# Masking x1 instead of the adjacency in a two-layer graph kernel, with other buffers and new orders

## Chip, core and metric

The kernel runs on one core of one Trainium2 chip. Its time is the device time of a run in microseconds (us); a version is described by the median of several runs. In the profile PE is TensorE (matmuls), PEld its weight load, DVE is VectorE, ACT is ScalarE, POOL is GpSimd and SP the engine that issues transfers. The operands of the products are 32-bit floats.

## What is computed

There are 64 graphs of 256 nodes with 512 features. Layer 0 averages the neighbours, multiplies by a weight and normalises; layer 1 scores each node by a product of queries and aggregated keys, takes a softmax of the scores over the nodes, adds the values so weighted, and normalises again.

```python
def layer0(x, adj, W):
    deg = jnp.sum(adj, axis=-1, keepdims=True)
    agg = jnp.einsum('bij,bjf->bif', adj, x) / jnp.maximum(deg, EPS)
    cat = jnp.concatenate([x, agg], axis=2)
    return jax.nn.relu(jnp.einsum('bnf,of->bno', cat, W))

def layer1(X, adj, mask, Wqk, Wv):
    q, k = jnp.split(X @ Wqk, 2, axis=-1)
    v = X @ Wv
    k_m = k * mask[:, :, None]
    agg = jnp.einsum('bij,bjd->bid', adj, k_m)
    w = inv_scale * mask * jnp.einsum('bid,bid->bi', q, agg)
    return jax.nn.softmax(w, axis=1)[:, :, None] * v

x = layernorm(x + layer0(x, adj, W))
x = layernorm(x + layer1(x, adj, nodemask, Wqk, Wv))
```

The mask stands on the node that is summed over: masking row j of the keys is the same as masking column j of the adjacency, or row j of x1, the input of layer 1, since the key weights can be multiplied in after the aggregation.

## The kernel before

Graphs go in pairs, 32 of them, and a loop over pairs j computes layer 0 of pair j together with layer 1 of pair j-1. Each product of 256x512 by 512x512, and each aggregation of 256x256 by 256x512, is done by Winograd's form of Strassen's method: seven products of half size and some sums of blocks on either side. Six of the seven weight products are split once more in the same way (seven matmuls of 256 columns), one is not (four matmuls of 512 columns, two for each graph).

Layer 0 consists of the products named i, k, m, p, q, r, s (`layer0`) and the gather a to g: the aggregation, applied to y, which is x times the second half of the weight. Layer 1 consists of J, K, H, Q, N, P, L (`layer1`), and the gather A to G, the aggregation of x1. The key weights were multiplied into the query weights at the start, so the scores are the dot product of q with the aggregate, and no product with keys remains. A gather needs the sums S1 to S4 of the adjacency (`adj_sums`, on GpSimd) and T1 to T4 of the other operand (`sums_T`, on VectorE). For layer 0, T1 of y comes out of the copy from PSUM (`split`), and T2 to T4 go to a buffer of their own, `tv`. For layer 1 the four T sums are made from x1 (`owns[j]`) and written to the first half of the buffer `shared` (`agg_of`). The aggregate takes the place of the T sums there, block by block, as the gather's matmuls have read them.

The mask is applied to the adjacency (`mask_adj`, four ScalarE instructions on 256 columns) once layer 0 has used it, and `adj_sums` is made a second time, from the masked adjacency, into the second of two buffers `sa`.

The buffer `turn` (`turned_rows`) has three uses in turn: rows of the adjacency, of which `degrees` takes the row sums on ScalarE (in place, two graphs by two halves); the transposed x1, which 16 transfers on SP's queue place in x1T (`norm0`, `place`); and the scores of all nodes on each partition, for the softmax.

The order of the work is made in two steps. `ORDER0` (first pair), `ORDER1` (second), `ORDER` (all others) and `ORDER9` (layer 1 of the last pair) name the TensorE units in the order in which they are recorded; `take` goes through them, and each `when` adds the work on other engines once the units that it names have been taken. An inner product has seven units, the whole one four, a gather unit has two matmuls, one for each graph. Then `Plan` arranges all recorded instructions anew: it has a cost for each, gives each a due time (TensorE's own position in the recorded order, and for the other engines what is needed for that), and lists, engine by engine, the ready instruction with the earliest due time. The program is issued in that order, and every engine then works through its list in order. `HOME` and `HOME9` name the PSUM bank in which a product or a gather unit works; the whole products use no such bank. `FULL_FIRST` and the like name products that are done whole at the start and the end. L is the last product of layer 1; `ahead` carries units of it from one pair to the next, if the order leaves some: with the strings of before it leaves none. `softmax` and the sums of layer 1 start when L is done (`start_layer1`).

All engine instructions have the line of one helper, 285 in the profile; matmuls have 370, transposes 376, transfers 386. Groups are told apart by the names of their tiles.

Of the kernel before, what the change touches and what calls it, by code (L numbers as in the profile page):

```python
# [13 lines left out]
OP = mybir.AluOpType  # L14
# [15 lines left out]
HOME = "i6 k7 m7 p2 q6 r7 s6 a7 b2 c3 J3 K2 H1 Q5 N7 L7 P7 A6 B4 C5"  # L30
HOME9 = "J1 K7 H3 Q7 N6 L1 P1 A2 B3 C1"
# [4 lines left out]
ORDER0 = ("k i k i k i i k i k i i k p k p m m m m q q s m m p p r r m r q r r r s r q a b s s d e c f g")  # L36
ORDER1 = ("i k i i k i i i i k k k p m m k k m m p m p q m m r p r r q r q q q q r q s r s s r s s a J J J "
          "J J s b s d e c J J f H K K H Q H K H K K K Q Q g N N K A N D P Q C E G N N N N P P L L L B L P "
          "L F L L")
ORDER = ("i k i i i k k i k i k i k m k p p p m m q m m r p r r m m r r r q q r q q q J q s J J s s s J J "  # L40
         "s a b d s s J e c J H f K K H K H g K K H K K Q Q A N Q N Q Q D N N C Q Q N P N E P N P P G P P "
         "P L F L B L L L L L")
ORDER9 = ("J J J J A J J C J D K B K K H K E H F G N H N H K Q Q K N P N N Q N Q N P K P P L S L Z L L")
# [277 lines left out]
def resnorm_kernel(  # L321
# [58 lines left out]
    def send(out, in_, due=None, late=0.0):  # L380
# [8 lines left out]
    (adjs, rows, xs, Xs, rdegs, sumsA, sumsM, owns, ys, aggs, vs, x1Ts, scores, columns, rows_w,  # L389
     probs) = ({} for _ in range(16))  # L390

    shared = mem.tile([P, 4 * N_SIDE], F32, name="shared")
# [4 lines left out]
    turned_rows = mem.tile([P, 2 * NT * F], F32, name="turn")  # L397
# [12 lines left out]
    def load_rows(j):  # L410
        rows[j] = turned_rows[:, :2 * NT * N].rearrange("p (k t n) -> p k t n", k=2, t=NT)
        for k in range(2):
            send(rows[j][:, k], adj[2 * j + k].rearrange("(t p) j -> p t j", p=P), late=LATE if j else 0.0)
# [113 lines left out]
    def adj_sums(j, n):  # L527
        a, s = adjs[j], sa[n]
# [6 lines left out]

    def mask_adj(j):
        for k in range(2):
            for t in range(NT):
                act.activation(adjs[j][:, k, t], adjs[j][:, k, t], AF.Copy,
                               scale=mask_sb[:, 2 * j + k, t:t + 1])  # L540
# [88 lines left out]
    def sums_T(val, to=None):  # L629
        b11, b12, b21, b22 = (val[:, :, t, h * HF:(h + 1) * HF] for t in range(NT) for h in range(2))  # L630
        if to is None:
            tv = ring("tv", [P, 3, 2, HF])
            t2, t3, t4 = (tv[:, r] for r in range(3))
            t1 = b12
        else:
# [512 lines left out]
```

## Time and profile before

| what | value |
|---|---|
| three runs | 1818.59, 1818.78, 1822.25 us; median 1818.78 |
| the profiled execution's own time | 1818.37 us |
| its span, first to last instruction | 1816.6 us |
| granted TensorE clock | 0.999 |
| HBM | 82 GB/s over the span |

The span is what the profile covers; the execution's own time is 1.8 us longer. Shares of busy time are means over the whole span: the first 110 us, in which weights are multiplied and summed and the pipeline fills, and the last 20 us, in which only one pair's layer 1 is left, look different from the loop between them. In a row of instruction groups the columns are line, engine, operation, output and inputs by name, shapes and count, then busy time in us and the mean of one in ns, then the idle time before them and what ended it. In an order of time the first two columns are the start and the duration in us; "x2" stands for two records, and a matmul on 32-bit floats has two.

The transfers of one pair in the loop, in order of time (start, duration over all that were merged, and how many):

```profile
499.55 11.26 SPq L386 DMA_DIRECT2D x1T<-turn  x16
510.91 0.56 SPq L386 DMA_DIRECT2D dram<-turned  x1
511.57 0.90 SPq L386 DMA_DIRECT2D turn<-adj  x2
513.25 0.37 SPq L386 DMA_DIRECT2D turn<-dram  x1
526.54 6.36 SPq L386 DMA_DIRECT2D xT<-x_t  x2
```

First the 16 that place x1T, then the scores' way through DRAM and the adjacency rows for the degrees of the next pair.

### The profile page before, as it was taken

What the parts mean: (1) busy time and instruction counts of PE and PEld (TensorE: products, weight loads), DVE (VectorE), ACT (ScalarE), POOL (GpSimd) and SP (SyncE); (2) the same over time, 40 slices, a digit from 0 to 9 for tenths busy, and PEclk for the clock granted to TensorE, in tenths of its full rate; (3) what the DMA queues carried; (4) which work ended last, traced back from release to release, by engine and by line L of the source; (5) the groups of instructions that cost most, each with busy time, mean ns of one, the idle gap of its engine ahead of it and who ended that gap; (6) DMA issues with size and microseconds to landing.
All of it is one profiled execution on the core that took longest, in us unless ns stands there. A gap on an engine that the chain in (4) does not pass through costs nothing.

```text
span 1816.6 us, 27899 instructions
## 1 busy us (share of the span) xinstructions
PE 1801.9 (99%) x7724; PEld 1439.9 (79%) x7724; DVE 1562.1 (86%) x3511; ACT 1299.2 (72%) x3475; POOL 1196.6 (66%) x1729
## 2 busy tenths in 40 slices
PE   9999999999999999999999999999999999999998
PEld 5777878878888888878788788888788887788875
DVE  7888888889888889898888898898888888988886
ACT  3657876678766778766787767787667777667866
POOL 5866676766766866766767667667667666676652
PEclk9999999999999999999999999999999999999999
DMA  7134334343243443343433433433434333334312
GB/s 239 52 77 116 94 94 100 99 111 101 86 117 87 101 118 95 91 112 88 111 104 97 104 88 100 122 94 88 119 81 111 106 104 95 97 92 120 94 20 77
DMA packets 380730, 181.72 MB, mean 100 GB/s; under 512 B 263712, under 2 KB 345248, under 8 KB 380576
## 3 DMA queue, kind: packets, MB, share of 16 engines
q1 hardware_dynamic: 380576, 179.94, 36.7%
q8 instruction: 63, 1.03, 0.3%
q14 instruction: 91, 0.75, 0.1%
HBM read 114.35 MB, written 34.08 MB: 82 GB/s over the span
## 4 chain that ended last, share of the span: by engine, by line
PE 98%; DVE 1%; DMA 1%; ACT 0%; SPq 0%; issue 0%; ACTq 0%; DVEq 0%
PE bank L370 98%; DMA shared<-wqk_t 1%; DVE bank L285 0%; PE bank L376 0%; DVE own L285 0%; SPq L386 0%; ACT own L285 0%; DVE t_i L285 0%; DVE st L285 0%; DVE w L285 0%; DVE x L285 0%; DVE y L285 0%; ACT y L285 0%; ACT shared L285 0%; DVE top L285 0%
## 5 line engine op out<-in xcount | busy, mean ns | idle before, releaser
L285 DVE TENSOR_TENSOR bank<-bank,fifth 128x256 f32<-128x256 f32 x866 | 377.9, 465 | 119.0 <-ACT fifth L285 83.1
L285 ACT COPY fifth<-bank 128x256 f32<-128x256 f32 x616 | 220.0, 373 | 234.1 <-PE bank L370 232.8
L285 ACT COPY y<-bank 128x512 f32<-128x512 f32 (+1 forms) x256 | 135.5, 532 | 130.8 <-PE bank L370 112.3
L370 PE MATMUL bank<-t_i,x1T_i 128*128 128x256 f32 x748 | 207.5, 379 | 1.1 <-ACT bank L285 1.1
L285 ACT COPY shared<-bank 128x512 f32<-128x512 f32 x314 | 179.8, 594 | 36.9 <-PE bank L370 34.8
L285 ACT ACTIVATE own<-own,shift,rstd 128x512 f32<-128x512 f32 x254 | 201.0, 828 | 0.2 <-DVE shift L285 0.2
L370 PE MATMUL bank<-t_i,xT_i 128*128 128x256 f32 x760 | 195.9, 379 | 0.0
L285 DVE SCALAR_TENSOR_TENSOR own<-bank,rdeg,own 128x256 f32<-128x256 f32 x384 | 172.2, 477 | 19.3 <-PE bank L370 17.0
L285 ACT ACTIVATE junk<-own,less 128x512 bf16<-128x512 f32 x254 | 184.0, 724 | 3.1
L285 ACT COPY bank<-bank 128x256 f32<-128x256 f32 (+1 forms) x352 | 145.9, 421 | 54.9 <-PE bank L370 35.8
L370 PEld LDWEIGHTS bank<-t_i,x1T_i 128*128 128x128 f32 x748 | 140.8, 190 | 35.6 <-issue 9.0
L285 DVE TENSOR_TENSOR y<-bank,y 128x512 f32<-128x512 f32 (+1 forms) x256 | 150.6, 618 | 20.2 <-PE bank L370 17.6
L370 PE MATMUL bank<-t,x1T_s 128*128 128x512 f32 (+1 forms) x384 | 163.5, 521 | 0.6 <-DVE own L285 0.6
L285 POOL TENSOR_TENSOR shift<-less,rstd 128x2 f32<-128x2 f32 x126 | 23.1, 203 | 212.9 <-ACT rstd L285 212.6
L370 PEld LDWEIGHTS bank<-t_i,xT_i 128*128 128x128 f32 x760 | 140.4, 189 | 27.4 <-issue 1.9
L370 PE MATMUL bank<-t,xT_s 128*128 128x512 f32 (+1 forms) x384 | 159.7, 521 | 0.0
L285 DVE TENSOR_TENSOR shared<-bank,shared 128x512 f32<-128x512 f32 (+1 forms) x157 | 138.4, 883 | 9.5 <-ACT shared L285 6.8
L285 POOL TENSOR_TENSOR x1T_i<-x1T 128x256 f32<-128x256 f32 x124 | 97.2, 793 | 74.8 <-PE bank L370 71.8
L370 PE MATMUL bank<-w,x1T_i 128*128 128x256 f32 x500 | 144.5, 380 | 0.5 <-DVE bank L285 0.5
L370 PE MATMUL bank<-w,xT_i 128*128 128x256 f32 x508 | 141.2, 380 | 0.6 <-DVE bank L285 0.5
L285 POOL TENSOR_TENSOR xT_s<-xT,xT_s 128x256 f32<-128x256 f32 x62 | 65.3, 1070 | 112.2 <-PE bank L370 110.8
L285 POOL TENSOR_TENSOR sa<-adj 128x256 f32<-128x256 f32 x128 | 92.1, 729 | 59.2 <-ACT adj L285 55.0
(174 smaller groups left out, 4788.5 us busy)
## 6 DMA issues: line engine op xcount, KB each, us to landing
x<-x SPq DMA_DIRECT2D x64, 512.0 KB, 3.4
xT<-x_t SPq DMA_DIRECT2D x62, 512.0 KB, 3.3
out<-own SPq DMA_DIRECT2D x62, 512.0 KB, 3.4
x1T<-turn SPq DMA_DIRECT2D x480, 64.0 KB, 2.1
turn<-adj SPq DMA_DIRECT2D x64, 256.0 KB, 3.3
adj<-adj_t SPq DMA_DIRECT2D x64, 256.0 KB, 3.5
turn<-dram SPq DMA_DIRECT2D x31, 264.0 KB, 5.1
shared<-wqk_t SPq DMA_DIRECT2D x4, 512.0 KB, 8.4
```

The source lines that it names most:

```text
L285: self.plan.record(self.name, lambda: call(out, *args, **kwargs), outs, ins, busy, done, port)
L370: plan.record("PE", lambda: nc.tensor.matmul(ps, a, b, start=start, stop=True, skip_group_check=True), [ps], [a, b], busy, busy + 0.165, w ...
```

## The change

- `mask_adj` and the second `adj_sums` are gone. `adj_sums` is made once for a pair, into one of the two buffers `sa` in turn, and used by both gathers.
- In their place `masked_T` masks x1: two ScalarE copies a graph write the masked blocks B11 (256 columns), and B21 with B22 (512 columns), to a new buffer `masked`. T1 is one VectorE instruction a graph (mask times block, less B11); T2, T3 and T4 are three GpSimd subtractions over both graphs. T still goes to the first half of `shared`. B12 isn't copied: T1 reads it from x1 itself and masks it on the way.
- `sums_T` now serves y alone, and its T2 to T4 go to the front of `turn` instead of `tv`, which is dropped. `turn` grows from 2048 to 2064 columns and the scores' row moves behind the T sums.
- The adjacency rows for the degrees go to `shared` (the first 1024 columns, the aggregate of one graph) from pair 3 on; those of pairs 0 to 2 stay in `turn`.
- `HOME` differs for p and H, which use no such bank. In `HOME9` J's bank changes from 1 to 7; H, Q, L and their like are whole there.
- New strings for all four orders. In `ORDER` the seven units of L are split: one is carried into the next pair, as its ninth unit. The first pairs' and the last one's orders differ in many places.

```diff
@@ -27,20 +27,20 @@
 W1_BY_GP = ("P5", "P3", "P4")
-HOME = "i6 k7 m7 p2 q6 r7 s6 a7 b2 c3 J3 K2 H1 Q5 N7 L7 P7 A6 B4 C5"
-HOME9 = "J1 K7 H3 Q7 N6 L1 P1 A2 B3 C1"
+HOME = "i6 k7 m7 p5 q6 r7 s6 a7 b2 c3 J3 K2 H4 Q5 N7 L7 P7 A6 B4 C5"
+HOME9 = "J7 K7 H2 Q5 N6 L7 P1 A2 B3 C1"
 LATE = 4.0
...
 FULL_FIRST = ("P7", "P4")
-ORDER0 = ("k i k i k i i k i k i i k p k p m m m m q q s m m p p r r m r q r r r s r q a b s s d e c f g")
-ORDER1 = ("i k i i k i i i i k k k p m m k k m m p m p q m m r p r r q r q q q q r q s r s s r s s a J J J "
-          "J J s b s d e c J J f H K K H Q H K H K K K Q Q g N N K A N D P Q C E G N N N N P P L L L B L P "
-          "L F L L")
-ORDER = ("i k i i i k k i k i k i k m k p p p m m q m m r p r r m m r r r q q r q q q J q s J J s s s J J "
-         "s a b d s s J e c J H f K K H K H g K K H K K Q Q A N Q N Q Q D N N C Q Q N P N E P N P P G P P "
-         "P L F L B L L L L L")
-ORDER9 = ("J J J J A J J C J D K B K K H K E H F G N H N H K Q Q K N P N N Q N Q N P K P P L S L Z L L")
+ORDER0 = ("i k i k k i i k k i i i p k k m m m p q m p p m r r q s r r q m r r r q s a s s m b d e c g f")
+ORDER1 = ("k k i k i i i i i k k k i m m m p k m p p m q p m m q r r r q r r r r q q q q s J a J s J s b J "
+          "J s s s s d J e c f J H H Q H K K K K Q H K g N N K Q Q P K N A D C E G B N N N N L P L L P L L "
+          "P F L")
+ORDER = ("i i i k k k k i L i k i k i m k p m m m p m q p p r r r r r m r m r q q q q q J q J s a J J s s "
+         "J s s s s J b d e c J f H K K K H H g K H K K K A Q N Q N Q N Q Q N Q C Q N P P P D E N F N P P "
+         "P G L P B L L L L L")
+ORDER9 = ("J J J C A J J D E B G N J N N J F H K H K N H Q Q K H K P Q N P K Q N K K P N P S L L Z L L")
@@ -386,15 +386,17 @@
-    (adjs, rows, xs, Xs, rdegs, sumsA, sumsM, owns, ys, aggs, vs, x1Ts, scores, columns, rows_w,
-     probs) = ({} for _ in range(16))
-
+    (adjs, rows, xs, Xs, rdegs, sumsA, owns, ys, aggs, vs, x1Ts, scores, columns, rows_w,
+     probs) = ({} for _ in range(15))
+
+    masked = mem.tile([P, 2, 3, HF], F32, name="masked")
     shared = mem.tile([P, 4 * N_SIDE], F32, name="shared")
...
                        for n in ("xT", "x1T"))
-    turned_rows = mem.tile([P, 2 * NT * F], F32, name="turn")
+    N_T, N_ROW = 3 * 2 * HF, P // Q * 2 * NT * (Q + 1)
+    turned_rows = mem.tile([P, N_T + N_ROW], F32, name="turn")
@@ -408,7 +410,7 @@
     def load_rows(j):
-        rows[j] = turned_rows[:, :2 * NT * N].rearrange("p (k t n) -> p k t n", k=2, t=NT)
+        rows[j] = (shared if j > 2 else turned_rows)[:, :2 * NT * N].rearrange("p (k t n) -> p k t n", k=2, t=NT)
         for k in range(2):
@@ -524,20 +526,14 @@
-    def adj_sums(j, n):
-        a, s = adjs[j], sa[n]
+    def adj_sums(j):
+        a, s = adjs[j], sa[j % 2]
         a11, a21, a12, a22 = (a[:, :, t, h * P:(h + 1) * P] for t in range(2) for h in range(2))
...
         return {"A11": a11, "A12": a12, "A22": a22, "S1": s[:, 0], "S2": s[:, 1], "S3": s[:, 2], "S4": s[:, 3]}
-
-    def mask_adj(j):
-        for k in range(2):
-            for t in range(NT):
-                act.activation(adjs[j][:, k, t], adjs[j][:, k, t], AF.Copy,
-                               scale=mask_sb[:, 2 * j + k, t:t + 1])
@@ -626,23 +622,30 @@
-    def sums_T(val, to=None):
+    def masked_T(j):
+
+        t1, t2, t4, t3 = (aggs[j][:, :, t, h * HF:(h + 1) * HF] for t in range(NT) for h in range(2))
+        b11, b21, b22 = (masked[:, :, r] for r in range(3))
+        x1 = owns[j]
+        for k in range(2):
+            m = mask_sb[:, 2 * j + k]
+            act.activation(b11[:, k], x1[:, k, 0, :HF], AF.Copy, scale=m[:, 0:1])
+            act.activation(masked[:, k, 1:].rearrange("p r f -> p (r f)"), x1[:, k, 1], AF.Copy, scale=m[:, 1:2])
+            vec.scalar_tensor_tensor(t1[:, k], x1[:, k, 0, HF:], m[:, 0:1], b11[:, k],
+                                     op0=OP.mult, op1=OP.subtract)
+        gp.tensor_sub(t2, b22, t1)
+        gp.tensor_sub(t3, t2, b11)
+        gp.tensor_sub(t4, b21, t2)
+        return {"B11": b11, "B21": b21, "B22": b22, "T1": t1, "T2": t2, "T3": t3, "T4": t4}
+
+    def sums_T(val):
         b11, b12, b21, b22 = (val[:, :, t, h * HF:(h + 1) * HF] for t in range(NT) for h in range(2))
-        if to is None:
-            tv = ring("tv", [P, 3, 2, HF])
-            t2, t3, t4 = (tv[:, r] for r in range(3))
-            t1 = b12
-        else:
-            t1, t2, t4, t3 = (to[:, :, t, h * HF:(h + 1) * HF] for t in range(NT) for h in range(2))
-        if to is not None:
-            vec.tensor_sub(t1, b12, b11)
-        vec.tensor_sub(t2, b22, t1)
-        if to is None:
-            vec.tensor_sub(t3, t2, b11)
-        else:
-            vec.tensor_sub(t3, b22, b12)
+        tv = turned_rows[:, :3 * 2 * HF].rearrange("p (r k f) -> p r k f", r=3, k=2)
+        t2, t3, t4 = (tv[:, r] for r in range(3))
+        vec.tensor_sub(t2, b22, b12)
+        vec.tensor_sub(t3, t2, b11)
         vec.tensor_sub(t4, b21, t2)
-        return {"B11": b11, "B21": b21, "B22": b22, "T1": t1, "T2": t2, "T3": t3, "T4": t4}
+        return {"B11": b11, "B21": b21, "B22": b22, "T1": b12, "T2": t2, "T3": t3, "T4": t4}
@@ -757,7 +760,7 @@
         x1Ts[j] = Side(home_x1, *sums_x1, 1, SLOTS_X1)
-        sq = turned_rows.rearrange("p (b k c t q) -> p b k c t q", b=P // Q, k=2, c=NF, t=NT)
+        sq = turned_rows[:, :2 * NT * F].rearrange("p (b k c t q) -> p b k c t q", b=P // Q, k=2, c=NF, t=NT)
@@ -793,7 +796,7 @@
         send(d, turned)
-        row = turned_rows[:, NT * F:NT * F + P // Q * 2 * NT * (Q + 1)].rearrange("p (a c) -> p a c", a=P // Q)
+        row = turned_rows[:, N_T:].rearrange("p (a c) -> p a c", a=P // Q)
         send(row, d.rearrange("(a c) q -> a c q", c=Q)[:, :2 * NT, :].rearrange("a c q -> a (c q)")
@@ -925,7 +928,7 @@
     inner_sums(Xs[0], "P2")
-    sumsA[0] = adj_sums(0, 0)
+    sumsA[0] = adj_sums(0)
     degrees(0)
@@ -947,12 +950,11 @@
         def start_gather0():
-            units.update(gather("abcdefg", sumsA.pop(j), sums_T(ys[j]), at["a"], at["c"], at["b"],
+            units.update(gather("abcdefg", sumsA[j], sums_T(ys[j]), at["a"], at["c"], at["b"],
                                 own=own, rdeg=rdegs.pop(j)))
...
             place = norm0(j)
-            mask_adj(j)
             if place:
@@ -974,7 +976,7 @@
                 load_adj(j + 1)
-                sumsA[j + 1] = adj_sums(j + 1, 0)
+                sumsA[j + 1] = adj_sums(j + 1)
         if j > 0:
@@ -1011,16 +1013,14 @@
                         turn_here(Y, owns[0], k, o)
-                    mask_adj(0)
                 else:
                     softmax(j - 2)
-                sumsM[j - 1] = adj_sums(j - 1, 1)
                 inner_sums(Y, None)
...
             def start_gather1():
-                units.update(gather("ABCDEFG", sumsM.pop(j - 1), T[0], at["A"], at["C"], at["B"],
+                units.update(gather("ABCDEFG", sumsA.pop(j - 1), T[0], at["A"], at["C"], at["B"],
                                     aggs[j - 1]))
@@ -1029,7 +1029,7 @@
             T = []
-            when("ikmpqrs" if j == 1 else "", lambda: T.append(sums_T(owns[j - 1], aggs[j - 1])))
+            when("ikmpqrs" if j == 1 else "", lambda: T.append(masked_T(j - 1)))
             when("gK", start_gather1)
@@ -1048,8 +1048,7 @@
     aggs[j] = agg_of(j)
-    T = sums_T(x1, aggs[j])
-    sumsM[j] = adj_sums(j, 1)
+    T = masked_T(j)
     turn_here(X, x1, 1, pw)
@@ -1057,7 +1056,7 @@
     units, dots = layer1(j, X, q_at, o, u, y, at)
-    units.update(gather("ABCDEFG", sumsM.pop(j), T, at["A"], at["C"], at["B"], aggs[j]))
+    units.update(gather("ABCDEFG", sumsA.pop(j), T, at["A"], at["C"], at["B"], aggs[j]))
     v = vs[j]
```

## The prediction

> **What bounds the kernel now.** I read the totals of the page first, then the chain of waits, then the busy time of each engine by stretches, and last the order of time around the places where TensorE stood still.
>
> ```profile
> span 1816.6 us, 27899 instructions
> ...
> PE 1801.9 (99%) x7724; PEld 1439.9 (79%) x7724; DVE 1562.1 (86%) x3511; ACT 1299.2 (72%) x3475; POOL 1196.6 (66%) x1729
> ...
> PE 98%; DVE 1%; DMA 1%; ACT 0%; SPq 0%; issue 0%; ACTq 0%; DVEq 0%
> ```
>
> TensorE is busy for 1801.9 of 1816.6 us and holds 98% of the chain that ended last. So 14.7 us is all that work off TensorE can give back, unless matmuls go; the change has the same matmuls (seven gather units of two matmuls before and after). The stretches say where the 14.7 us lie:
>
> ```profile
> core 0: us, PE busy (x) PEld busy (x) DVE busy (x) ACT busy (x) POOL busy (x), PEclk, DMA share, GB/s
> 0.00:55.00 55.00, 52.79 (x172) 31.73 (x173) 41.11 (x74) 22.04 (x62) 35.00 (x50) 1.00 0.66 221
> 55.00:110.00 55.00, 51.56 (x209) 36.80 (x209) 46.59 (x92) 34.29 (x81) 37.83 (x52) 1.00 0.12 39
> ...
> 495.00:550.00 55.00, 55.00 (x240) 44.69 (x239) 47.98 (x109) 40.20 (x110) 37.06 (x54) 1.00 0.39 102
> 525.00:535.00 10.00, 10.00 (x44) 8.03 (x43) 9.91 (x26) 8.64 (x27) 0.87 (x3) 1.00 0.28 96
> ...
> 1760.00:1816.60 56.60, 47.68 (x200) 34.52 (x198) 39.13 (x92) 42.15 (x109) 14.70 (x26) 0.96 0.19 61
> ```
>
> Idle TensorE: 2.2 us in the first stretch, 3.4 in the second, 8.9 in the last, 0 in a stretch of the steady loop. A busy TensorE isn't TensorE at its peak, so its pace counts too. The same matmul of two successive pairs starts at
>
> ```profile
> 500.32 0.59 PE L370 MATMUL bank<-own,sa 128*128 128x256 f32 x2
> ...
> 555.64 0.59 PE L370 MATMUL bank<-own,sa 128*128 128x256 f32 x2
> ```
>
> a period of 55.32 us. In the order of time, starts of 256-column matmuls run from 537.51 to 544.85 in 17 steps, 0.432 us each; two 512-column ones stand between 44.74 and 46.46, 0.86 each. A pair needs, for each of two layers, six products of 7 small matmuls, one of 4 large, and 14 small for the gather: 2 x (56 x 0.432 + 4 x 0.86) = 55.26. So 0.1 us a pair is lost: 29 like pairs, at most 3 us. The 3.4 us of the second stretch are four waits, while the pipeline fills:
>
> ```profile
> 89.65 0.70 PE L370 MATMUL bank<-tv,adj 128*128 128x256 f32 x2 [1.25 <-DVE own L285]
> 90.93 0.70 PE L370 MATMUL bank<-t,x1T_s 128*128 128x256 f32 x2 [0.58 <-DVE own L285]
> ...
> 93.01 1.13 PE L370 MATMUL bank<-w,x1T_i 128*128 128x256 f32 x4 [0.53 <-DVE bank L285]
> 95.23 0.67 PE L370 MATMUL bank<-t_i,x1T_i 128*128 128x256 f32 x2 [1.09 <-ACT bank L285]
> ```
>
> **The change, by pair of graphs.** Durations are these groups':
>
> ```profile
> L285 DVE SCALAR_TENSOR_TENSOR own<-bank,rdeg,own 128x256 f32<-128x256 f32 x384 | 172.2, 477 | 19.3 <-PE bank L370 17.0 <-ACT own L285 0.9
> ...
> L285 POOL TENSOR_TENSOR sa<-adj 128x256 f32<-128x256 f32 x128 | 92.1, 729 | 59.2 <-ACT adj L285 55.0 <-PE bank L370 4.2
> ...
> L285 ACT ACTIVATE adj<-adj,mask_sb 128x256 f32<-128x256 f32 x132 | 67.5, 517 | 3.6 <-PE bank L370 3.2
> ...
> L285 DVE TENSOR_TENSOR shared<-own 128x512 f32<-128x512 f32 x64 | 44.9, 701 | 1.8
> ...
> L285 POOL TENSOR_TENSOR x1T_s<-x1T 128x512 f32<-128x512 f32 x31 | 39.6, 1278 | 0.3 <-ACT x1T L285 0.3
> ```
>
> Removed: on ScalarE four maskings, 4 x 0.517 = 2.07 us; on GpSimd the second set of four adjacency sums, 0.729 x 2 + 0.737 + 0.781 = 2.98; on VectorE four T sums, 2 x 0.701 + 2 x 0.736 = 2.87.
>
> Added: on ScalarE four masked copies, two of 256 columns at 0.517 and two of 512. For the latter the rows give 0.594 (a plain copy of 512 from PSUM) to 0.828 (the scaling of own, two column operands); a copy grows by 0.22 from 256 to 512, so 0.517 + 0.22 = 0.74. Sum 2.51, **+0.44 a pair**. On VectorE two scalar_tensor_tensor of 256 columns, nearest row 0.477: 0.95, **-1.92**; if each is doubled by a wait, as "tv<-y" shows (minimum 0.681, median 1.372), still -1.0. On GpSimd three subtractions of 512 columns: 1.278 each where undisturbed, 1.653 in the row "x1T_s<-x1T_s,x1T": 3.83 to 4.96; I take the first, since two subtractions of that length stand undisturbed in each pair: **+0.85**.
>
> None of the three engines sets the end of a steady pair (48.0, 40.2 and 37.1 of 55), so I cost these at nothing; what hides them is TensorE's 55. GpSimd has the room in one piece: 0.87 busy in 525 to 535.
>
> One rule speaks against the move. The Trainium skill, "Perfetto Trace Analysis", section "Optimizing Scalar/DVE Operations", says that moving work between VectorE and GpSimd might not help, as they share a read port. The trace shows the price: 1.278 on GpSimd against 0.701, and "tv<-y" at twice its minimum. By the rule VectorE's -1.92 would come to nothing; by the rows about -1.9 stays; either way the end isn't touched.
>
> **Moved buffers.** From the fourth pair on, the adjacency rows for the degrees land in the first half of the aggregate, where T is built. So for one of the two graphs T1 waits for the degrees of the next pair, behind which the chain is: dots that read the aggregate end at 505.4; the two row transfers issue at 511.57, behind the 16 that place x1T (from 499.55, 11.26 us); they land about 3.3 us later; ScalarE's degrees ended at 525.95. Then T1 (0.95) and three subtractions (3.83): 530.8. GpSimd's own next work, "shift", starts at 533.40; the first matmul that reads a T sum is "shared,sa" at 543.98. That leaves 13 us; with 1.653 for each subtraction, 12. Cost nothing; if the rows were 14 us late, each further one would cost 29.
>
> T sums of y now wait for the "turn" buffer. In the loop it is free at about 513 (placing ended at 510.8, and about 2 us to land), they start at 521.1: 8 us of cover. In the first pair they started at 41.23, while the degrees of the second pair, in the same buffer, ran from 42.12 to 43.8. Those rows were issued at 23.09, and ScalarE is busy 22 of the first 55 us, so the degrees can go earlier: 0, at most 2.6 us. The reload for the third pair then waits until TensorE has read the sums (49.7 instead of 43.8); its degrees are used an iteration later.
>
> **Orders.** The four strings are priorities: instructions are listed by what is ready, so matmuls next to each other in a string needn't wait for each other. In the new loop one unit of product L is carried into the next pair, and layer 1's start waits for it: it ends after nine units, 9 x 0.43 = 3.9 us. The sums that follow also need the 16 transfers that place x1T, which take 11.26 us to issue; so nothing. Fill: from -3.4 (all four waits gone) to +3.4 (doubled), its own row being all I have. The weight load before the wait at 95.23 is put down to GpSimd's "t_i"; GpSimd loses four sums in this stage and gets its T work later (the T sums stood at 100.0 to 107.3). I credit that wait alone: -1.1. Loop: from -2.9 (nothing lost) to what rival two costs; VectorE is nearly full where hand-offs are closest and loses 1.92, so a third: -1.0. Tail (the one wait there was 0.9): -0.9 to +0.9, taken as 0.
>
> Sum on the profiled execution's own time: 1818.37 (its span of 1816.6 and 1.8 around it) - 1.1 - 1.0 = 1816.3; the median of the runs is 0.4 above that execution: **1816.7**.
>
> **Rivals.** One, *hand-offs cleared*: fill, loop and tail waits all go: -3.4 - 2.9 - 0.9 = -7.2, 1811.6. For it: everything lost is hand-offs, and VectorE, which releases most of them, gets lighter. Against: they are latencies from one engine to the next, not queues.
>
> Two, *VectorE's full stretch*: T1 must follow the degrees, which ended at 525.95, and VectorE is busy 9.91 us of the 10 from 525 on. Of 0.95 us, 0.09 fits; up to 0.86 pushes evictions that TensorE waits for. Above 0.13 us a pair (29 pairs, 3.6 us) it decides; at half of 0.86, 29 x 0.43 = +12.5: 1831. Against: the 2.87 us taken out stood at 501.9 to 508.2, and T1 can be ordered after 535 with 8 us to spare.
>
> Three, *a longer fill*: the first pair's wait of 2.6 and twice the 3.4: +6.0, 1824.8.
>
> **How the numbers follow.** What a measurement of this kernel can tell from no change is 0.2%, 3.6 us. Forecast 0.50, 1813 to 1821, of it 0.17 below 1815.1 and 0.33 within. Rival one 0.17. Rival two 0.25, three 0.08. So faster 0.34, same 0.33, slower 0.33. Low end 1810, below rival one's value, leaving 0.05 out; the top must take in rival three and the part of rival two up to 0.3 us a pair (8.7): 1826, leaving about 0.13 out.
>
> **What would show it.** Right: period 55.2 to 55.35 us, TensorE 55 of 55 in the loop, ScalarE up 0.4, VectorE down 1.9, GpSimd up 0.9 a pair; the wait near 95 us gone. Rival two: a TensorE wait "<-DVE" once a pair, just after the degrees. Wrong altogether: a matmul reading the new T sums and waiting for GpSimd, or transfers of x1T landing later.

## The result and the profile after

The changed kernel takes 1822.49 us (median of 20 runs, 1821.95 to 1823.18); the kernel before, beside it, 1818.72 (20 runs). The ratio is 1.0018, interval 1.0012 to 1.0023: 3.8 us slower, about the 0.2% that a measurement can tell, where 2 us faster was forecast. The profiled execution took 1822.13 us, its span is 1820.4; that of before was 1816.6. The page of the changed kernel, engines' totals and the chain of waits:

```profile
span 1820.4 us, 27722 instructions
...
PE 1806.7 (99%) x7724; PEld 1441.5 (79%) x7724; DVE 1499.8 (82%) x3447; ACT 1322.4 (73%) x3471; POOL 1197.5 (66%) x1697
...
PE 97%; DVE 1%; ACT 1%; DMA 1%; issue 0%; SPq 0%; POOL 0%; ACTq 0%; DVEq 0%
```

TensorE has the same 7724 matmuls and is still 97% of the chain. VectorE has 62 us less to do, and yet TensorE's busy time grew by 4.8 us: matmuls that wait a little are counted as longer ones. Busy time by stretches, the changed kernel (columns as shown before):

```profile
55.00:110.00 55.00, 54.52 (x224) 39.57 (x224) 48.63 (x100) 37.34 (x95) 38.94 (x50) 1.00 0.14 45
110.00:165.00 55.00, 54.04 (x231) 42.53 (x230) 44.96 (x101) 37.49 (x103) 36.91 (x53) 1.00 0.29 75
...
330.00:1595.00 1265.00, 1264.88 (x5469) 1024.58 (x5468) 1051.78 (x2442) 941.65 (x2481) 849.33 (x1205) 1.00 0.38 101
```

and the loop of the kernel before:

```profile
330.00:1595.00 1265.00, 1265.00 (x5487) 1027.20 (x5486) 1104.62 (x2497) 924.58 (x2489) 852.39 (x1230) 1.00 0.38 102
```

From 55 to 110 us TensorE gained 3 us of busy time (51.56 before). From 110 to 165 it lost 1 (55.00 before). The loop, 330 to 1595, looks full, as before, but holds 5469 matmuls in place of 5487. At 0.216 us for one record of 256 columns, 18 of them are 3.9 us. So the loss is in the loop, where busy time can't show it. The same matmul of two successive pairs, in the changed kernel's order of time:

```profile
512.75 0.66 PE L370 MATMUL bank<-w,xT_s 128*128 128x256 f32 x2
...
568.25 0.66 PE L370 MATMUL bank<-w,xT_s 128*128 128x256 f32 x2
```

The period is 55.50 us, against 55.32 before; over the 21 periods between 346 and 1512 us its mean is 55.50, and single ones are 55.46 to 55.51 with two exceptions (55.74, 55.62).

To see where it goes, I took the starts of TensorE's records and summed what each interval has above its usual pace (0.216 us after a record of 256 columns, 0.429 after one of 512, 0.109 after one of 128). These "lost" microseconds by region (us of the span), for the kernels before and changed and for the experiments below whose loops stay near theirs:

| kernel | 0-60 | 60-110 | 110-165 | 165-330 | 330-1600 | 1600-1772 | after | median of runs |
|---|---|---|---|---|---|---|---|---|
| before | 2.8 | 5.15 | 0.6 | 1.0 | 2.6 | 1.2 | 1.8 | 1818.7 |
| changed | 3.2 | 1.9 | 2.2 | 1.0 | 6.8 | 0.85 | 2.2 | 1822.5 |
| e1 new code, old strings | 3.3 | 1.3 | 2.2 | 0.95 | 6.7 | 6.0 | 4.1 | 1830.5 |
| e2 old code, new strings | 3.4 | 4.25 | 0.6 | 1.4 | 3.4 | 7.75 | 2.5 | 1829.3 |
| e3 old code, new fill | 3.7 | 4.2 | 0.6 | 1.9 | 2.6 | 1.2 | 1.8 | 1818.7 |
| e6 T on GpSimd, order kept | 2.8 | 5.1 | 0.9 | 1.7 | 2.5 | 6.6 | 1.9 | 1827.2 |
| e7 changed, order kept, less work | 3.7 | 1.2 | 2.2 | 1.0 | 7.0 | 0.8 | 2.2 | 1821.9 |
| e8 changed, first block ahead | 3.4 | 4.2 | 1.7 | 3.7 | 18.2 | 3.35 | 2.3 | 1840.8 |
| e9 before, other constants | 2.65 | 2.9 | 0.8 | 1.5 | 2.9 | 1.6 | 1.8 | 1817.6 |
| e10 changed, other constants | 3.3 | 1.6 | 1.6 | 1.2 | 7.0 | 0.9 | 2.3 | 1821.3 |
| e12 changed, short additions | 3.3 | 1.9 | 1.4 | 0.9 | 5.4 | 0.35 | 2.2 | 1819.4 |

The granted clock stood at half for 6.8 us of e1's profiled execution (from 1747.5 us) and for 3.4 us of e2's (1613.1) and e3's (95.6), and the 1.4 to 2.8 us that TensorE lost in each are not in the table; executions of the kernel before with a lower mean clock (0.996 for 0.998 or 0.999, up to 8 of 21 beside an experiment) take some 3.8 us more, which moves the ratios below more than the medians, and none of the changed kernel's 20 has one.

Changed less before: fill -3.2, the next stretch +1.6, the loop +4.2, the rest +0.5: +3.1; and from the last matmul's start to the end of the span there are 9.2 us instead of 8.6. That is the 3.8 us of the spans.

Within the loop, the waits of TensorE's weight loads between 500 and 555 us (who waited for what, total us, times, longest), the kernel before:

```profile
PEld bank L370 <- DVE bank L285: 2.1, 7, 0.4
PEld bank L370 <- issue: 2.1, 9, 0.2
```

and the changed kernel:

```profile
PEld bank L370 <- issue: 2.8, 11, 0.4
PEld bank L370 <- DVE bank L285: 1.0, 4, 0.3
PEld bank L370 <- POOL xT_i L285: 0.4, 2, 0.2
PEld bank L370 <- ACT fifth L285: 0.2, 1, 0.2
```

The reader should see two things. Waits for VectorE are halved, part of which a lighter VectorE brings (1.4 us in 4 waits in e6 below, under the list of before); and new ones stand beside them, for ScalarE, GpSimd and "issue". None is for a T sum. Most weights are loaded 0.2 us ahead of their matmul (525.62 for the one at 525.84), so a wait of that length need not delay it. The places where a matmul did start late, in the order of time of the changed kernel, the pair from 457 us and the next:

```profile
468.65 1.03 PE L370 MATMUL bank<-turn,sa 128*128 128x256 f32 x4
469.51 0.59 PE L370 MATMUL bank<-w,x1T_i 128*128 128x256 f32 x2
469.75 0.57 ACT L285 COPY bank<-bank 128x512 f32<-128x512 f32 x1
469.94 0.59 PE L370 MATMUL bank<-t,xT 128*128 128x256 f32 x2
470.38 0.30 PEld L370 LDWEIGHTS bank<-y,sa 128*128 128x128 f32 x2 [0.24 <-ACT bank L285]
470.38 0.70 PE L370 MATMUL bank<-y,sa 128*128 128x256 f32 x2
...
521.85 0.30 PEld L370 LDWEIGHTS bank<-t_i,xT_i 128*128 128x128 f32 x2 [0.19 <-ACT fifth L285]
521.89 0.65 PE L370 MATMUL bank<-t_i,xT_i 128*128 128x256 f32 x2
...
524.31 0.43 DVE L285 TENSOR_TENSOR bank<-bank,fifth 128x256 f32<-128x256 f32 x1 [0.32 <-PE bank L370]
524.65 0.87 DVE L285 SCALAR_TENSOR_TENSOR own<-bank,rdeg,own 128x256 f32<-128x256 f32 x2
525.63 0.85 ACT L285 COPY bank<-bank 128x512 f32<-128x512 f32 x2 [0.52 <-DVE total L285]
526.34 1.10 PE L370 MATMUL bank<-y,sa 128*128 128x256 f32 x4
```

A pair of matmuls at full pace has 0.59 in the second column; 0.65 or 0.70 means that the second or the next was late. The product of y and sa slips by 0.10 us in the one pair and 0.15 in the other, each time 0.63 to 0.71 us after ScalarE's copy to a bank began; the product of t_i and xT_i slips by 0.06 in each. In the kernel before the same ScalarE copies start at 525.86 and the product only at 526.74, 0.88 us later and at full pace:

```profile
524.58 1.03 PE L370 MATMUL bank<-tv,sa 128*128 128x256 f32 x4
525.44 0.59 PE L370 MATMUL bank<-w,x1T_i 128*128 128x256 f32 x2
525.86 0.85 ACT L285 COPY bank<-bank 128x512 f32<-128x512 f32 x2
525.87 0.59 PE L370 MATMUL bank<-t,xT 128*128 128x256 f32 x2
526.30 0.59 PE L370 MATMUL bank<-t,xT_i 128*128 128x256 f32 x2
526.74 1.03 PE L370 MATMUL bank<-y,sa 128*128 128x256 f32 x4
```

Here less lies between. The copy takes up the product of the T sums and sa, so it can't start before that product ends. In the kernel before three products stand between that one and the product of y and sa, in each pair. In the changed kernel's first pair only two do, and the copy starts 0.07 us after the end (469.68). In its second pair there are three, but the copy starts late, behind VectorE. Where the 4.2 us of the loop lie follows from the starts that come more than 0.02 us late between 330 and 1600 us: y and sa 3.1 us (34 times) and t_i and xT_i 1.3 (22 times), neither of them late in the kernel before; w and xT_s 1.5, as before (1.6); the others 0.4, as before (0.4, at t and xT_i).

### The profile page after: what moved, and what is told of

The parts are those of the page before. It is cut to its first block, busy times and chain, and to the rows that moved or that the text cites. A ratio compares the mean times of both kernels' runs of the same rounds, so it can differ in the third digit from the quotient of the medians.

```text
span 1820.4 us, 27722 instructions
## 1 busy us (share of the span) xinstructions
PE 1806.7 (99%) x7724; PEld 1441.5 (79%) x7724; DVE 1499.8 (82%) x3447; ACT 1322.4 (73%) x3471; POOL 1197.5 (66%) x1697
## 4 chain that ended last, share of the span: by engine, by line
PE 97%; DVE 1%; ACT 1%; DMA 1%; issue 0%; SPq 0%; POOL 0%; ACTq 0%; DVEq 0%
PE bank L370 97%; DMA shared<-wqk_t 1%; DVE own L285 0%; DVE bank L285 0%; ACT junk L285 0%; PE bank L376 0%; SPq L386 0%; ACT fifth L285 0%; ACT own L285 0%; ACT bank L285 0%; DVE t_i L285 0%; DVE y L285 0%; DVE st L285 0%; ACT y L285 0%; DVE w L285 0%
## 5 line engine op out<-in xcount | busy, mean ns | idle before, releaser
L285 DVE TENSOR_TENSOR bank<-bank,fifth 128x256 f32<-128x256 f32 x866 | 383.9, 466 | 121.1 <-ACT fifth L285 83.0
L370 PE MATMUL bank<-t_i,x1T_i 128*128 128x256 f32 x748 | 202.8, 380 | 0.2 <-DVE shared L285 0.2
L370 PE MATMUL bank<-t_i,xT_i 128*128 128x256 f32 x760 | 201.6, 381 | 0.0
L285 ACT ACTIVATE own<-own,shift,rstd 128x512 f32<-128x512 f32 x254 | 197.2, 816 | 1.2 <-POOL shift L285 0.9
L285 POOL TENSOR_TENSOR xT_s<-xT,xT_s 128x256 f32<-128x256 f32 x62 | 45.1, 727 | 192.1 <-PE bank L370 190.4
L370 PE MATMUL bank<-w,x1T_i 128*128 128x256 f32 x500 | 149.0, 380 | 1.0 <-DVE bank L285 0.6
L285 ACT COPY own<-bank 128x512 f32<-128x512 f32 x192 | 110.2, 589 | 45.5 <-PE bank L370 36.2
```

Of the source, the lines that this page charges most:

```text
L285: self.plan.record(self.name, lambda: call(out, *args, **kwargs), outs, ins, busy, done, port)
L370: plan.record("PE", lambda: nc.tensor.matmul(ps, a, b, start=start, stop=True, skip_group_check=True), [ps], [a, b], busy, busy + 0.165, w ...
```

## The experiments

Theory one, arrangement: the kernel's `Plan` lists all instructions anew whenever code, buffers or strings differ, and what TensorE loses at hand-overs follows from that list. Theory two, load: the added GpSimd work, the moved buffers or the carried unit of L cost the time themselves. Theory three, strings: the new orders do it.

**Code or strings.** e1 is the changed kernel with all six strings of before, e2 the kernel before with all six new ones, e3 the kernel before with the new `ORDER0` and `ORDER1` (and an L added at its end, since nothing is carried). Of the strings only the first line of `ORDER` in e1, and of `ORDER0` in e2 and e3, is shown.

```diff
-ORDER = ("i i i k k k k i L i k i k i m k p m m m p m q p p r r r r r m r m r q q q q q J q J s a J J s s "
+ORDER = ("i k i i i k k i k i k i k m k p p p m m q m m r p r r m m r r r q q r q q q J q s J J s s s J J "
...
-ORDER0 = ("k i k i k i i k i k i i k p k p m m m m q q s m m p p r r m r q r r r s r q a b s s d e c f g")
+ORDER0 = ("i k i k k i i k k i i i p k k m m m p q m p p m r r q s r r q m r r r q s a s s m b d e c g f")
...
```

> The changed kernel with the four order strings and the bank lists of before (masked x1, T sums on GpSimd and the moved buffers stay). Theory 'strings': the new strings make the loop lose 0.17 us a pair; with the old ones the period is 55.31 us again, TensorE's waits between 330 and 1600 us return from 6.8 to about 2.6 us, and the time falls to about 1818. Theory 'code': the listing of the loop follows from the instructions and buffers, not from the strings; the period stays at 55.48 to 55.50 us and only the fill and the tail change, so the time stays at 1821 to 1826.

> The kernel of before with the four new strings and bank lists (masked adjacency, T sums on VectorE, old buffers stay). Theory 'strings': period 55.48 us in the loop. Theory 'code': period 55.31 us in the loop as before; what changes lies in the fill (the waits at 88 to 98 us, 3.4 us of idle TensorE, become shorter if the strings are what shortened them) and at the end, where the strings were not made for this code and may cost some us.

> The kernel of before with the new strings for the first two pairs only (with the one unit of L that the new second string leaves taken at its end). If the shorter fill of the changed kernel comes from the strings, TensorE's idle time from 55 to 110 us falls from 3.4 to under 2 and the time is 1 to 3 us below before, with a period of 55.31 us. If it comes from the lighter engines, the fill stays at 3.4 and the time at 1818.7.

Measured: e1 1830.53 us, ratio to before 1.0061 (1.0048 to 1.0074); e2 1829.28, 1.0053 (1.0040 to 1.0065); e3 1818.74, 0.9994 (0.9985 to 1.0003). e1 lies above both of its forecasts, by what it lost at the end. In the table the loop follows the code: 6.7 with new code and old strings, 3.4 with old code and new strings. So does most of the shorter fill: 1.3 in e1, 4.2 in e2 and e3. The late products of e1's loop are those of the changed kernel (2.8 us at y and sa, 1.6 at t_i and xT_i). What the strings decide is the end. Each half alone loses 6 to 8 us there, as e2's stretches show:

```profile
330.00:1595.00 1265.00, 1265.00 (x5484) 1026.41 (x5483) 1102.52 (x2496) 923.02 (x2484) 846.91 (x1228) 1.00 0.38 101
1595.00:1760.00 165.00, 160.03 (x681) 127.50 (x680) 136.44 (x303) 112.42 (x293) 104.51 (x153) 0.99 0.33 86
```

The loop has 5484 matmuls, near the 5487 of before; the stretch behind it lost 5 us, where before lost none. The new strings are matched to the new code, not better by themselves. Theory three falls for the loop, and with it the carried unit of L, which e1 doesn't have.

**Which engine makes T.** e4 is the changed kernel with its three subtractions on VectorE, e5 the kernel before with T2 to T4 of x1 on GpSimd; both are arranged anew.

```diff
-        gp.tensor_sub(t2, b22, t1)
-        gp.tensor_sub(t3, t2, b11)
-        gp.tensor_sub(t4, b21, t2)
+        vec.tensor_sub(t2, b22, t1)
+        vec.tensor_sub(t3, t2, b11)
+        vec.tensor_sub(t4, b21, t2)
```

```diff
+        eng = vec if to is None else gp
...
-        vec.tensor_sub(t2, b22, t1)
...
+        eng.tensor_sub(t2, b22, t1)
+        eng.tensor_sub(t3, t2, b11)
+        eng.tensor_sub(t4, b21, t2)
```

> The changed kernel with T2, T3 and T4 of x1 on VectorE in place of GpSimd, all else the same. VectorE gets 3 x 0.7 = 2.1 us a pair more, GpSimd 3.8 less. Theory 'full stretch' (T comes after the degrees, where VectorE has no room, and GpSimd is what saves the change): TensorE's loss in the loop rises to 1 us a pair or more, the time by 30 us or more. Theory 'T on GpSimd is what is late': the period falls to 55.31 and the time to about 1818.

> The kernel of before (old strings, masked adjacency, old buffers) with T2, T3 and T4 of x1 on GpSimd in place of VectorE, arranged anew by the planner. Theory 'load': VectorE loses 2.2 us a pair, GpSimd gains 3.8 and has the room, so the period stays at 55.3 us and the time at 1819 (or below). Theory 'arrangement': any edit sends the loop into another arrangement, whose lost time has little to do with the work moved; the period moves by 0.2 us a pair or more, the time by 6 us or more.

Measured: e4 1890.51, ratio 1.0390 (1.0374 to 1.0406); e5 1904.55, 1.0464 (1.0450 to 1.0479). In the loop TensorE is busy 1223.4 and 1233.3 us of 1265. Moving the work to VectorE cost the changed kernel 68 us, moving it to GpSimd cost the kernel before 86. Two opposite moves that both cost so much are no price of a subtraction. Both runs have a new list as well as another engine, so they can't tell the two apart; the next two hold the list still.

**The same list, other work.** In e6 the kernel before keeps its list, made for VectorE, and the T subtractions are only issued on GpSimd. In e7 the changed kernel keeps its list, but the maskings and T2 to T4 are left out.

```diff
+        def sub(out, c, d):
+            vec.tensor_sub(out, c, d)
+            if to is not None:
+                plan.steps[-1].issue = lambda: nc.gpsimd.tensor_sub(out, c, d)
...
-        vec.tensor_sub(t2, b22, t1)
+        sub(t2, b22, t1)
```

and for e7, with the matmuls of the gather reading x1 itself in place of what is left out:

```diff
+        def instead(issue):
+            plan.steps[-1].issue = issue
...
+            instead(lambda k=k, m=m: nc.vector.scalar_tensor_tensor(
+                t1[:, k], x1[:, k, 0, HF:], m[:, 0:1], c11[:, k], op0=OP.mult, op1=OP.subtract))
...
+        instead(None)
```

> The same three subtractions on GpSimd, but the list of instructions is made as if they were on VectorE and kept, so that every engine works through what it had in the order of before. Theory 'arrangement': the three GpSimd instructions are not what costs; the loss is far below that of the same edit arranged anew, at most the subtractions' extra length where something waits behind them. Theory 'load' has the same time as there.

> The changed kernel with its list of instructions kept, but without the four masked copies on ScalarE and the three T subtractions on GpSimd: the gather's matmuls read x1 and T1 in their place. It leaves out the mask and T2 to T4, so it does 2.5 us a pair less on ScalarE and 3.8 less on GpSimd, and nothing else changes its place. Theory 'arrangement': the loop still loses what it lost, 0.17 us a pair over before (period 55.48 us, TensorE's waits from 330 to 1600 us near 6.8). Theory 'added work' (the port that GpSimd and VectorE share, or ScalarE's copies, hold up evictions): the period falls to 55.31 us and the time by 4 us.

Measured: e6 1827.19, 1.0037 (1.0024 to 1.0049); e7 1821.89, 1.0009 (1.0000 to 1.0017). First e6's stretches and the rows of its GpSimd subtractions:

```profile
330.00:1595.00 1265.00, 1265.00 (x5488) 1029.70 (x5487) 1052.66 (x2429) 924.04 (x2488) 924.31 (x1299) 1.00 0.38 102
1595.00:1760.00 165.00, 161.08 (x693) 128.22 (x692) 136.44 (x303) 110.33 (x290) 115.00 (x164) 1.00 0.33 83
```

```profile
L640 POOL TENSOR_TENSOR shared<-own,shared 128x512 f32<-128x512 f32 x64 | 81.4, 1271 | 55.2 <-DVE wide L285 45.2 <-DVE shared L285 8.1 <-DVE turned L285 1.8
...
L640 POOL TENSOR_TENSOR shared<-own 128x512 f32<-128x512 f32 x32 | 40.7, 1271 | 34.8 <-DVE bank L285 33.5 <-ACT own L285 1.3
```

In the loop VectorE does 52 us less than before and GpSimd 72 more, and TensorE does exactly what it did: 5488 matmuls. Its period is 55.30 us. Load there costs nothing, and relief brings nothing. The profiled execution, 1825.37 us, is the shortest of the five, so this accounts for 6.5 of the 8.2 us by which the medians differ. In it e6 is slower at the end alone, 1600 to 1772 us, presumably since a list made for VectorE's shorter subtractions is no longer met; the largest waits of TensorE there, in its order of time:

```profile
1738.98 1.13 PE L370 MATMUL bank<-w,xT_i 128*128 128x256 f32 x4 [0.73 <-POOL xT_i L285]
1747.20 0.70 PE L370 MATMUL bank<-tv,sa 128*128 128x256 f32 x2 [1.48 <-DVE tv L285]
1749.07 0.70 PE L370 MATMUL bank<-w,x1T_i 128*128 128x256 f32 x2 [1.18 <-DVE bank L285]
```

e7 is the mirror: GpSimd has 81 us less to do in the loop (768.31 of 1265 instead of 849.33), ScalarE 49 less, and the period stays at 55.47 to 55.51, with two exceptions (55.67, 55.79). The loop loses 7.0, as with the work, and at the same two products (2.8 and 1.6 us). For the loop theory two falls, as far as it means the added work of GpSimd and ScalarE. The moved buffers stand in e7 as well; no run moves them under a list held still. The changed kernel's own trace speaks against them: between 330 and 1600 us no instruction waited for one that works on `turn`, the two late products read neither `turn` nor `shared`, and the product of turn and sa, whose copy the first of them needs, is itself on time. e5 and e6 also show what a list is worth: the same three subtractions on GpSimd (but for the operands of T3) take 77 us more where the list was made anew.

**The late product.** e8 tries the hand-over itself: in the changed kernel's list the scaled additions of the gather's first block go ahead of two other VectorE instructions.

```diff
+AHEAD = 2
...
+            while passed < AHEAD and all(t is not s for t, _ in listed[at - 1].next):
+                at -= 1
+                passed += listed[at].engine == "DVE" and not listed[at].first
...
+                plan.steps[-1].first = (t, h) == (0, 0)
```

> The changed kernel with its list kept but for one thing: in each gather of layer 0 the two VectorE instructions that empty the bank c (so that ScalarE can write it again and the matmuls with S4 can follow) are put ahead of up to two additions of 'fifth' that stood in front of them. If the wait of those matmuls (0.10 to 0.15 us a pair at 'bank<-y,sa') comes from VectorE's order, it goes: 3 to 4 us over the loop, 1818.5 to 1819.5 in all. If the additions that are now later make other matmuls wait as long, the time stays at 1822.5.

Measured 1840.82, ratio 1.0113 (1.0097 to 1.0128): a miss. The loop lost 18.2 instead of 6.8, and between 500 and 555 us the weight loads waited more for VectorE's additions to a bank (1.4 us in 5 waits against 1.0 in 4); over the run matmuls waited 16 times, 9.3 us, for "own", a row that the changed kernel does not have. What is put behind on VectorE makes other matmuls late. The order of that one hand-over was no free gain, and whether the chain sets the slip stayed open.

e12 therefore leaves the list as it is and makes the instruction in question shorter.

```diff
+                plan.steps[-1].issue = lambda r=r[:, :32], p=ps[:, k * HF:k * HF + 32], d=rdeg[:, k, t:t + 1]: (
+                    nc.vector.scalar_tensor_tensor(r, p, d, r, op0=OP.mult, op1=OP.add))
```

> The changed kernel in its own order of every engine, but each of the 384 scaled additions of the gather into own takes 32 of its 256 columns (the other columns' message is left out), so that VectorE is done with the bank about 0.3 us earlier at each. Question: what makes TensorE slip by 0.10 to 0.15 us at the product of y and sa, 526.34 us, in every pair. Theory one, the chain of hand-offs there: addition of the fifth product (524.31), scaled additions into own (524.65, 0.87 us for two), ScalarE's copy to the bank (525.63, which waited 0.52 for VectorE), product (526.34); then this slip goes, the period falls from 55.49 to about 55.37 us and the waits over 330 to 1600 us from 6.8 to about 3.5 to 4; 1818.5 to 1820. Theory two, the slip has another cause (the copies of the fifth product on ScalarE, GpSimd's xT_i): the waits stay at 6.3 to 7 us and the time at 1821.5 to 1822.5, since VectorE had room everywhere else.

Measured 1819.44, ratio to before 0.9994 (0.9984 to 1.0004); the loop lost 5.4. The period is now 55.52 in one pair and 55.35 in the next, in turn. e12's order of time, both pairs:

```profile
469.24 0.30 PEld L370 LDWEIGHTS bank<-y,sa 128*128 128x128 f32 x2 [0.24 <-ACT bank L285]
469.24 0.70 PE L370 MATMUL bank<-y,sa 128*128 128x256 f32 x2
...
523.57 0.40 DVE L661 SCALAR_TENSOR_TENSOR own<-bank,rdeg,own 128x32 f32<-128x32 f32 x2
524.13 0.57 ACT L285 COPY bank<-bank 128x512 f32<-128x512 f32 x1
524.75 0.59 PE L370 MATMUL bank<-w,x1T 128*128 128x256 f32 x2
525.18 1.03 PE L370 MATMUL bank<-y,sa 128*128 128x256 f32 x4
```

In the second pair the two additions take 0.40 us instead of 0.87, the copy starts 0.56 after them, and the product follows the matmul before it at the full pace (525.18 after 524.75): the slip of 0.15 is gone. There theory one of that run is shown. In the first pair the slip of 0.10 stays: ScalarE's copy again starts 0.62 ahead of the product (468.62 and 469.24). It follows the end of the product of turn and sa (468.54), not VectorE, and two products instead of three stand behind that one, in e12's list too. A new slip of 0.05 shows at 483.57. So the forecast loss of 3.5 to 4 was too low: the chain named makes the product late in every second pair only (over the loop y and sa are late by 1.1 us in place of 3.1). The rest of e12's gain, about 1.3 us, lies from 110 to 165 us and at the end, where the shorter additions help too.

**The list alone.** e9 and e10 change three constants of `Plan` each and nothing else; e11 makes one part of the change alone in the kernel before, the buffers.

```diff
-    SLACK = {"PE": 0.06, "DVE": 0.12, "ACT": 0.12, "POOL": 0.12, "SP": 0.1}
+    SLACK = {"PE": 0.04, "DVE": 0.12, "ACT": 0.12, "POOL": 0.13, "SP": 0.1}
...
-                    if e == "PE" and at > free[e] - 0.15:
+                    if e == "PE" and at > free[e] - 0.1:
```

```diff
-    SLOW = {"DVE": 1.04, "ACT": 1.04, "POOL": 1.04}
+    SLOW = {"DVE": 1.04, "ACT": 1.035, "POOL": 1.04}
...
-            s.due = min(s.due, self.clock + 6.0)
+            s.due = min(s.due, self.clock + 5.5)
...
-                        at += 0.08
+                        at += 0.07
```

> The kernel before with not one instruction, buffer or order string changed: only three constants by which its planner lists the work (the slack that it gives TensorE's operations 0.04 in place of 0.06, GpSimd's 0.13 in place of 0.12, and the threshold under which a matmul is taken to follow at once 0.1 in place of 0.15). Theory one, arrangement: what a kernel of this family loses is set by how the list falls out. The same 7724 matmuls then lose another amount, and most of what can move is the 5.15 us that TensorE lost between 60 and 110 us in the kernel before; if the new listing leaves 2 us there and the loop as it is (2.6 us over 330 to 1600), the time is about 3 to 4 us less, 1814.5 to 1816. Theory two, load: the time follows from what each engine is given to do, which is the same to the instruction, so 1818.7 and no more than 1 us away from it.

> The changed kernel, again with only three constants of its planner changed (the horizon of due times 5.5 in place of 6.0, the step added to a matmul that has to wait 0.07 in place of 0.08, ScalarE's allowance 1.035 in place of 1.04). Theory one, arrangement: the 0.15 us a pair that the changed kernel lost more than the kernel before between 330 and 1600 us is a matter of the list and can shrink with it, as can the 2 us between 110 and 165; with half of the loop's 6.8 us and most of the 2 us gone, about 1817 to 1819, so about as fast as the kernel before or faster. Theory two, load: the three subtractions on GpSimd and the other buffers cost this much wherever they are listed, so 1822 to 1823 as the changed kernel.

```diff
-        rows[j] = turned_rows[:, :2 * NT * N].rearrange("p (k t n) -> p k t n", k=2, t=NT)
+        rows[j] = (shared if j > 2 else turned_rows)[:, :2 * NT * N].rearrange("p (k t n) -> p k t n", k=2, t=NT)
...
-            tv = ring("tv", [P, 3, 2, HF])
+            tv = turned_rows[:, :3 * 2 * HF].rearrange("p (r k f) -> p r k f", r=3, k=2)
```

> The kernel before with one part of the change alone: the T sums of y in turn instead of a ring of their own, the degree rows of the later pairs in shared, turn made larger for it; masked adjacency, all subtractions and the order strings as before. Theory one, arrangement: buffers that come free at other times make the planner list the loop anew, as a change of engine did; order strings that were made for another list then cost several us or tens of us, 1825 to 1860, and the loop's waits over 330 to 1600 us are well above 2.6 us though every engine does the same work. Theory two, load: no instruction is added or made longer, so 1818 to 1821 at most by the waits for the shared buffers themselves, which would stand as waits for VectorE's subtractions into turn and for the copies of the rows.

Measured: e9 1817.62, ratio 0.9982 (0.9974 to 0.9991); e10 1821.26, 1.0007 (0.9998 to 1.0016); e11 1873.17, 1.0289 (1.0275 to 1.0303). e9 beats both kernels, by 1.6 us and some 5 (1.2 and 4.9 by the spans), with the instructions of before; it gains 2.2 in the fill, as expected, and gives 1.3 back in small pieces behind it. So its forecast had the mechanism and was 2 us too bold. e10 is a miss for both theories: its loop still loses 7.0, and of the 0.9 us by which its span is shorter 0.6 lie behind the last matmul. Other constants made another list, with other late products: over the loop y and sa are late by 0.7 us in place of 3.1, but t_i and xT_i by 2.1, t and xT by 1.2 and y and adj by 0.8, and its period is 55.78 and 55.23 in turn. So which products are late is a matter of the list; that their sum stayed is not explained. e11, above even the 1825 to 1860 of its forecast, shows what the buffers do together with the list that they bring about. Its stretch of the loop:

```profile
330.00:1595.00 1265.00, 1246.74 (x5311) 987.48 (x5310) 1084.40 (x2410) 906.65 (x2419) 826.02 (x1199) 1.00 0.36 98
```

By the sum of the table TensorE loses 45 us in the loop, with the work of before, instruction for instruction. Of those who waited for the buffer `turn` (who, total us, times), ScalarE's longest row and TensorE's two are

```profile
  ACT shared L285: 11.7, 10
...
  PEld bank L370: 1.8, 3
  PE bank L370: 1.5, 3
```

TensorE's are 3.3 us in the whole run, and none of them lies between 330 and 1600 us. There ScalarE, GpSimd and VectorE waited 22 us for it, and what of that was passed on to TensorE isn't shown; all of it would be half of the 45. So waits of TensorE for `turn` don't account for the 54 us. How much is the list and how much the buffers' own waits, e11 can't tell, since both are new in it.

## Why the prediction was wrong, point by point

**What bounds the kernel** held: TensorE, same matmuls, 14.7 us to gain at most.

**The load of the other engines** held. The new instructions, in the changed kernel's groups:

```profile
L285 POOL TENSOR_TENSOR shared<-masked,shared 128x512 f32<-128x512 f32 x64 | 82.7, 1293 | 16.6 <-DVE shared L285 6.8 <-ACT own L285 5.2 <-ACT rstd L285 4.6
...
L285 ACT ACTIVATE masked<-own,mask_sb 128x512 f32<-128x512 f32 x64 | 43.3, 717 | 1.4
...
L285 DVE SCALAR_TENSOR_TENSOR shared<-own,mask_sb,masked 128x256 f32<-128x256 f32 x64 | 37.1, 580 | 0.2
```

Copies of 0.511 and 0.717 (0.517 and 0.74 estimated), subtractions of 1.27 to 1.29 (1.278), T1 0.58 (0.477). Over the page VectorE has 1.95 us a pair less (62.3 / 32; 1.92 forecast), ScalarE 0.7 more (0.44). GpSimd's total is unchanged instead of 0.85 up, so that sign of being right failed: other sums of its own got shorter, such as "xT_s<-xT,xT_s", 1.07 to 0.73. The rule cited there, that a move from VectorE to GpSimd might not help, was right about the time and not for its reason: VectorE did become lighter, here and in e6.

**Moved buffers** held as far as they were costed: T1 and the subtractions come at 541.76 to 546.39, and the first reader, at 546.26, isn't held up by them. In the loop nothing waited for `turn`. In the first pair T of y started 0.24 us later than before, and its first product was not late. That these moves would make another list of everything else was not thought of; e11 shows what the two together can be worth.

**The fill**, credited with -1.1, gave -3.2, and 1.6 came back between 110 and 165: -1.6 net. The wait at 95 us is gone, as said. **The tail** and the first pair, taken as 0, cost 1.1 (0.6 behind the last matmul, 0.5 in TensorE's lost time).

**The loop is the step that failed**: "VectorE is nearly full where hand-offs are closest and loses 1.92, so a third: -1.0". It came to +4.2. Waits for VectorE did get shorter, 2.1 to 1.0 us between 500 and 555. But the step took the arrangement as fixed and gave the lighter engine the credit, with a share, a third, that no row gave. What the loop loses is a few hand-overs a pair that miss by 0.06 to 0.15 us, and which ones miss is settled when the list is made. The runs show it from four sides: with the list held, taking 52 us off VectorE changed nothing (e6: 2.5 us lost in the loop, 2.6 before), nor did taking work off GpSimd and ScalarE (e7: 7.0 and 6.8); another list with the same work is late at other products (e10); shortening one hand-over took one slip away (e12). That the new list comes from the moved buffers, and not from the masking, is not shown.

**Rivals.** Hand-offs cleared: no. VectorE's full stretch: its sum was wide enough (+12.5) but its place was wrong: T1 stands at 504.67 and 541.76, outside of it, and without the T work (e7 leaves out all but T1) the loss is the same. Near its place ScalarE's copy does wait for VectorE in every second pair (525.63), but for additions that the kernel before has too. A longer fill: the opposite. The rival that was missing is a loop arranged anew that misses more hand-overs.

**Signs of right and wrong.** "TensorE 55 of 55 in the loop" came true and told nothing; the period did (55.2 to 55.35 forecast, 55.50 measured).

Open: which part of the edit made the planner put two products instead of three in front of the product of y and sa in every second pair, and whether a list without the late products exists for the changed code; e10 is one try. The slip of 0.06 at t_i and xT_i, which waits for ScalarE's "fifth", was not tried by itself.

## What to carry to other kernels

Where a program lists the instructions, an edit is two edits: the work that it changes and the list that it changes everywhere. Cost them apart, and test them apart by issuing other work under the old list, since here the second was worth some 4 us in the changed kernel and 77 between e5 and e6, and the first, in the loop, nothing. In a kernel whose main engine reads as full, compare the period of one named instruction and the count of matmuls in a stretch, not busy time.

## What was not expected of the hardware

TensorE's busy time rose by 4.8 us with the same 7724 matmuls at the same granted clock (0.999): a matmul whose second record, or whose successor, comes late is recorded as a longer one (0.65 to 0.70 us for two records, in place of 0.59), and a stretch reads as full while it loses time. And 52 us less on VectorE in the loop with 72 more on GpSimd (e6) moved TensorE there by nothing that the trace resolves.
